# Group-norm statistics of layers 0 to 2 on ScalarE, layer 2's normalisation on ScalarE, and the quantiser's two steps swapped

## The chip, the cores and the metric

The kernel runs on one core of one Trainium2 chip. That core has a matrix engine (TensorE, "PE" in the profile), a vector engine (VectorE, "DVE"), a scalar engine (ScalarE, "ACT"), a general-purpose engine (GpSimd, "POOL", which does almost nothing here) and DMA queues, of which this kernel uses the one that SyncE ("SP") issues. Each engine takes its instructions in the order in which the program lists them and waits for the others by semaphores. The metric is the device time of one launch in microseconds, the median of three runs.

## The reference, cut to what matters

Eight images of 32 channels and 256 x 256 pixels in float32 go through four layers. Each adds its output to its input; the first three work on a group-normalised copy of it (16 groups of two channels, mean and variance over the whole image).

```
x: (8, 32, 256, 256) float32
def gn(v):  m, s = mean, var over each group of 2 channels;  return (v - m) / sqrt(s + 1e-5)

# layer 0: 1x1 convolution, then a depthwise 5x5 convolution whose weights are
#          the convolved feature map itself, average-pooled to 5x5
f = conv1x1(gn(x), w0) + b0;   x = x + depthwise5x5(f, adaptive_pool_5x5(f))
# layer 1: quantised "adder" convolution
q = round(clip(gn(x) / 2**-7, -127, 127));   wq = the same with the weights' own scale
x = x + -sum_{c, 3x3} |q patch - wq| * 2**-7        # for each of 32 outputs
# layer 2: 3x3 convolution
x = x + conv3x3(gn(x), w2) + b2
# layer 3: windows of 8x8, layernorm y, three small networks on three arrangements of y
#          (each: layernorm, eight Gaussians exp(-((v - g_k)/d)**2) times weights, plus
#          silu(v) times weights), their sum z, and a fourth such network on z
x = x + fastkan4(z) + z's residual
```

## The kernel before, in words

A pixel plane is cut into four bands of 64 rows; a tile has 128 partitions, band times channel. A chunk is eight rows of each band: 128 x 2048 values (`F` = 2048), eight chunks an image.

**Stage 0** (layer 0, from line 710). For each of eight chunks: a load from `x`, four `bn_stats` on DVE (`add_stats`, L618, the instruction is at L624) and five row sums for the pooled weights (L730). `Norm.finish` (L628) joins the statistics: `bn_aggr` (L637), two or three tiny matmuls across partitions, and a chain of small DVE operations. Then again for each chunk: a load with a border of two rows, 25 taps on PE (L873) and their edge corrections into the PSUM buffer `psB`, an eviction by ACT (L906), `bn_stats` for layer 1's normalisation, a store to `x1`. At the end eight tiles are scaled on ACT (L948), clipped (L953) and rounded to bf16 (L954) on DVE, and stored to `q`.

**Stage 1** (layer 1, L1008). Sixteen passes an image, one for each quarter of the rows and each group of eight output channels. A pass makes 72 distance tiles of 128 x 4128 values, max(q - w, 0), on DVE (L977) or, in halves, on ACT (L979), and PE sums each into the PSUM buffer `psA` (`gather`, L999: eight matmuls); nine more gathers take the plain sums, and one product adds the residual `xr` (L988). ACT evicts `psA` into `xr` (L1046), two `bn_stats` take the statistics for layer 2, a store goes to `x2`. Distance tiles have three buffers, `dv`.

**Stage 2** (layer 2, L1071). For each chunk: a load of ten rows, normalisation on DVE (`normal`, L1112), nine taps into `psB` (L1129), eviction by ACT (L1145), `bn_stats` for layer 3, a store to `x3`.

**Stage 3** (layer 3, L1170). Eight units an image, each one chunk through four networks. A network takes eight times a Square (L1368) and an Exp (L1381) on ACT and a product with weights on PE (L593) into `psB`; before it come a centring, a variance and a scaling that also go through PSUM (L1219, L1224, L1232, L1264, L1272). Line 1449 evicts the last network of a unit, so it runs 64 times.

**The order of the work** is made by a planner in the kernel itself (`Plan.run`, L228). It is a list schedule that runs while the program is built: every task has an engine, a cost in us, a rank (image plus a fraction) and buffers to be had, and a free engine takes the ready task of lowest rank. The time from one engine's end to another's start is `LAT`. Distances and gathers are not tasks but fillers (`fill`, L346; `Pass.piece`, L379; `on_pe`, L404): PE takes a gather ahead of all tasks when two distance tiles are waiting for it (`URGENT`), the other engines take a distance when no task is ready, and ACT only when it has had no task for 8 us (`IDLE`) or the image is the first. What comes out is one fixed instruction order for each engine. Ranks let stage 0 of later images, the passes of one image, and stages 2 and 3 of the image before run together. After the last pass, DVE may take Squares of stage 3 from ACT (L1374). The fixed memory `arena` (kind `sb`, ten times `F` words) holds most tiles; a load of a later image is only placed when five times `F` words stay free beyond its own (`FUTURE`).

```
            if self.sums and len(self.queue) < URGENT and (late or not (urgent or self.queue)):
                t, us, bufs, n = self.sums.pop(0), 0.53, [], 1
```

## Time and profile before

| | us |
|---|---|
| median of three runs (15972.1 to 15999.17) | 15973.13 |
| the profiled execution, its own time | 15969.78 |
| span in the profile, first to last instruction | 15967.3 |
| DVE busy | 13454.6 (84%) |
| PE busy | 12928.0 (81%) |
| ACT busy | 12386.4 (78%) |
| mean granted PE clock | 0.92 of full |
| DMA | mean 123 GB/s |

A busy time is the union of an engine's instructions. A row of the profile's groups names line, engine, operation and tiles ("out<-in"), the count, the busy time in us and the mean ns of one, and then the engine's idle time just ahead of such instructions with what ended it. The waits say who waited for whom: total us, times, longest. The windows give busy time in a stretch of the span, with the number of instructions behind an x.

The execution has five stretches, which show in the starts of the evictions at lines 1046, 1145 and 1449. Up to about 435 us there is only stage 0 of image 0. From there to 1,871 us come image 0's sixteen passes, beside stage 0 of images 1 to 3. To about 8,000 us the passes of images 1 to 4 run beside stage 3 of images 0 to 2 and stage 0 of the rest. To 14,602 us, the end of the last pass, stage 0 is over; passes run beside stages 2 and 3. The rest, 1,365 us, is the last of image 6's stage 3 (to 14,715 us) and then stages 2 and 3 of image 7 alone.

### The profile page before, as it was taken

To read this page: it belongs to the slowest core of one execution; us is meant where nothing else is said; L and a number is where in the kernel's file an instruction comes from. 1 tells how busy PE (TensorE), PEld (TensorE's weight loads), DVE (VectorE), ACT (ScalarE), POOL (GpSimd) and SP (SyncE) were. 2 spreads that over 40 slices of the span, in tenths; PEclk is the share of its full clock that TensorE was granted. 3 is DMA by queue.
4 is the path that set the end of the run, shared out by engine and by line. 5 is a ranking of instruction groups with operands and counts; after the bars stand their busy time and mean duration, and the time that the engine had idled before them with its cause. 6 is when DMAs were issued, how large, how long until landed. Compare 5 with 4: busy or idle time off the path is not lost. (4 is left out here: it accounts for less than half of the span.)

```text
span 15967.3 us, 560619 instructions
## 1 busy us (share of the span) xinstructions
PE 12928.0 (81%) x260296; PEld 4325.8 (27%) x260296; DVE 13454.6 (84%) x12544; ACT 12386.4 (78%) x6843; POOL 16.7 (0%) x25
## 2 busy tenths in 40 slices
PE   5889887987887888788887888788878888877666
PEld 4333322222332222232222222222222222222222
DVE  2889889898878889888999988999898989897465
ACT  0899749678658766866888987899779987997687
POOL 0000000000000000000000000000000000000000
PEclk8989899999999999899999999899999999998777
DMA  4332446445445444643554454444544454444554
GB/s 117 78 96 54 105 113 169 109 107 153 130 101 152 126 112 120 166 106 105 152 132 123 126 134 122 122 123 127 127 126 126 126 122 138 116 132 114 144 154 130
DMA packets 1192870, 1970.85 MB, mean 123 GB/s; under 512 B 362752, under 2 KB 878848, under 8 KB 1092224
## 3 DMA queue, kind: packets, MB, share of 16 engines
q1 hardware_dynamic: 1190528, 1934.98, 46.1%
q8 instruction: 2036, 33.36, 0.9%
q14 instruction: 306, 2.51, 0.1%
HBM read 1162.83 MB, written 771.75 MB: 121 GB/s over the span
## 5 line engine op out<-in xcount | busy, mean ns | idle before, releaser
L977 DVE TENSOR_SCALAR dv<-qh,w1q 128x4128 bf16<-128x4128 bf16 (+1 forms) x8831 | 10521.9, 1248 | 1376.3 <-PE psA L999 1319.3
L999 PE MATMUL psA<-dv,sel_b 128*32 128x512 bf16 x71240 | 5434.0, 405 | 1339.6 <-DVE dv L977 1054.2
L999 PEld LDWEIGHTS <-sel_b 128*32 128x32 bf16 x82944 | 2053.9, 97 | 6792.6 <-issue 5786.5
L1368 ACT ACTIVATE bas<-arena,kb 128x2048 f32<-128x2048 f32 x1386 | 2762.3, 1993 | 408.3 <-DVE arena L1272 262.9
L1381 ACT ACTIVATE bas<-bas 128x2048 f32<-128x2048 f32 x1386 | 2653.1, 1914 | 39.0
L979 ACT ACTIVATE dv<-qh,w1n 128x2064 bf16<-128x2064 bf16 x827 | 1628.6, 2009 | 1126.8 <-PE psA L999 1035.3
L593 PE MATMUL psB<-bas,tl 32*32 32x512 f32 x48416 | 1955.5, 652 | 491.1 <-ACT bas L1381 247.6
L873 PE MATMUL psB<-arena,wt 32*32 32x512 f32 (+1 forms) x51040 | 1848.5, 607 | 99.5 <-issue 61.4
L593 PE MATMUL psB<-arena,tl 32*32 32x512 f32 x22496 | 909.4, 621 | 161.7 <-ACT si L1449 46.1
L593 PEld LDWEIGHTS psB<-bas,tl 32*32 32x32 f32 x48416 | 535.2, 107 | 1384.3 <-ACT bas L1381 518.8
L873 PEld LDWEIGHTS psB<-arena,wt 32*32 32x32 f32 x51040 | 651.2, 104 | 778.1 <-issue 607.1
L1368 ACT ACTIVATE arena<-arena,kb 128x2048 f32<-128x2048 f32 x410 | 816.1, 1991 | 0.0
L1381 ACT ACTIVATE arena<-arena 128x2048 f32<-128x2048 f32 x410 | 785.0, 1915 | 12.3
L624 DVE BATCH_NORM_STATS2 tiny<-arena 128x6 f32<-128x512 f32 x768 | 473.5, 679 | 351.8 <-ACT arena L906 246.0
L999 PE MATMUL psA<-qh,sel_b 128*32 128x512 bf16 x9216 | 672.2, 393 | 92.3 <-DMA qh<-q 77.9
L1447 ACT ACTIVATE si<-psB,cols_sb 128x2048 f32<-128x2048 f32 x192 | 377.4, 1966 | 453.3 <-PE psB L593 369.9
L1272 DVE TENSOR_TENSOR arena<-psB,arena 128x2048 f32<-128x2048 f32 x280 | 640.5, 2287 | 86.2 <-PE psB L1264 79.2
L593 PE MATMUL psB<-si,tl 32*32 32x512 f32 x14080 | 630.6, 624 | 48.8 <-ACT si L1447 19.5
L1129 PE MATMUL psB<-arena,tl 32*32 32x512 f32 (+3 forms) x16384 | 626.6, 608 | 14.7 <-issue 14.4
L1224 ACT ACTIVATE arena<-arena 128x2048 f32<-128x2048 f32 x320 | 612.7, 1915 | 15.7 <-DMA x<-arena 5.8
L1264 PE MATMUL psB<-rs,tl 32*32 32x512 f32 x8960 | 338.9, 630 | 222.5 <-DVE arena L1272 128.2
L906 ACT ACTIVATE arena<-psB,cc 128x2048 f32<-128x2048 f32 x64 | 125.7, 1964 | 493.2 <-PE psB L894 493.2
(151 smaller groups left out, 7686.6 us busy)
## 6 DMA issues: line engine op xcount, KB each, us to landing
arena<-x SPq DMA_DIRECT2D x128, 1024.0 KB
arena<-y SPq DMA_DIRECT2D x128, 1024.0 KB
si<-sy SPq DMA_DIRECT2D x512, 256.0 KB
arena<-in_x_dram SPq DMA_DIRECT2D x240, 384.0 KB
arena<-in_x_dram SPq DMA_DIRECT2D x256, 256.0 KB
x<-arena SPq DMA_DIRECT2D x256, 256.0 KB
xr<-x SPq DMA_DIRECT2D x512, 128.0 KB
x<-xr SPq DMA_DIRECT2D x512, 128.0 KB
```

The source lines that it names most:

```text
L593: nc.tensor.matmul(o[j * C : (j + 1) * C, i - first, :], w_, src(rows, i, j), start=start, stop=stop)
L624: nc.vector.bn_stats(self.stats[:, at + i, :], a[:, i * 512 : (i + 1) * 512])
L873: nc.tensor.matmul(o[:, lo - 2 * j : hi - 2 * j, c0:c1], wt[rows, t, :], d[rows, lo + dy + 2 : hi + dy + 2, c0 + dx : c1 + dx], start=firs ...
L977: nc.vector.tensor_scalar(dst, src, w1q[:, at : at + 1], 0.0, ALU.subtract, ALU.max)
L979: nc.scalar.activation(dst, src, AF.Relu, bias=w1n[:, at : at + 1])
L999: nc.tensor.matmul(psA[j * C : (j + 1) * C, i, :], sel_b[:, n, :], src[:, at : at + 2, t % 3 : t % 3 + W], **flags,)
L1129: nc.tensor.matmul(o[:, lo - 2 * j : hi - 2 * j, c0:c1], (wc if t == 4 else tl[:, W2T + t, :])[rows], d[rows, lo + dy + 1 : hi + dy + 1, c ...
L1224: plan.add("ACT", 1.9, lambda: nc.scalar.activation(sb(sq), sb(c), AF.Square), r=[c], w=[sq], rank=rk)
L1272: lambda ps=ps, at=at: nc.vector.tensor_tensor(sb(c)[:, at], ps().rearrange("p s f -> p (s f)"), sb(c)[:, at], ALU.mult),
L1368: lambda k=k, bas=bas: nc.scalar.activation(sb(bas), sb(rb), AF.Square, bias=kb[:, n, k : k + 1]),
L1381: lambda k=k, bas=bas, square=square: nc.scalar.activation(sb(bas), sb(bas), AF.Exp, scale=-1.0, bias=0.0 if square.eng == "ACT" else kbsq ...
L1447: nc.scalar.activation(sb(o), psB.rearrange("p s f -> p (s f)"), AF.Identity, bias=obias)
```

## The change

**Statistics.** For the normalisations of layers 0, 1, 2 and 3 (every use of `bn_stats`), the sum is now taken by the instruction that writes the tile, where ACT writes it: the evictions at L906, L1046 and L1145 get `accum_out`. In stage 0's first part, where no ACT instruction writes the tile, DVE adds up the row sums that it makes anyway and takes off the columns that two bins share: three small operations. The sum of squares comes from a new ACT pass for each tile, `add_squares`: Square with a per-partition bias (minus the mean of the first tile, made by one small DVE operation for each group of tiles) and an accumulator; its elementwise output is bf16 waste, written behind the tile's data. So tiles get half as much room again: stage 0's first loads take 12 rows' worth instead of 8, stage 2's tiles 12 instead of 10, `xr` three quarters of `F` instead of half. `finish` replaces `bn_aggr` by six small DVE operations.

**Normalisation of layer 2.** `normal` is an Identity activation on ACT with scale and bias per partition, instead of a DVE `tensor_scalar`; one small DVE operation makes the bias.

**Quantiser.** DVE first rounds float32 to bf16 and then clips bf16 in place, instead of clipping in float32 and then rounding to bf16.

**Planner.** `LAT` grows by 0.03 to 0.05 us; a gather is costed at 0.49 instead of 0.53 us; PE pays 0.05 us in the plan each time it changes between fillers and tasks; tasks moved to ACT have costs there. A new rule lets PE take a gather instead of a task whose rank is over 9.0 (`AHEAD`) past the image of the current pass.

```diff
-ROOM = [("bas", 3 * BASE, BASE), ("si", 3 * F, F), ("rs", F // 2, F // 4), ("xr", F // 2, F // 2), ("sb", 10 * F, 0)]
+ROOM = [("bas", 3 * BASE, BASE), ("si", 3 * F, F), ("rs", F // 2, F // 4), ("xr", 3 * F // 4, 3 * F // 4), ("sb", 10 * F, 0)]
+AHEAD = 9.0
...
-    LAT = {"PE": 0.15, "DVE": 0.12, "ACT": 0.25, "SP": 2.0}
+    LAT = {"PE": 0.2, "DVE": 0.15, "ACT": 0.3, "SP": 2.0}
...
+                        if best is not None and e == "PE" and best.rank > self.image() + AHEAD:
+                            piece = self.fill(e, False)
+                            if piece is not None:
+                                best = piece
+                        if best is not None and best.n is not None:
...
+                    if e == "PE":
+                        us += 0.05 * ((t.n is None) != self.filling)
+                        self.filling = t.n is None
...
+    def image(self):
+        return next((p.b for p in self.passes[self.first_pass :] if not p.done), len(self.passes))
...
         if self.sums and len(self.queue) < URGENT and (late or not (urgent or self.queue)):
-            t, us, bufs, n = self.sums.pop(0), 0.53, [], 1
...
-            us, bufs, n = 0.53, [d], 1
+            us, bufs, n = 0.49, [d], 1
...
+            self.sums, self.squares, self.shift = t[:, 0:16], t[:, 16:32], t[:, 32 : 32 + n]
+            self.summed = Buf("fixed")
+            self.chunks, self.shifted = 0, [Buf("fixed") for _ in range(n)]
...
+        def add_squares(self, src, at, i, size, rank):
+
+            if not self.chunks & 1 << i:
+                self.chunks |= 1 << i
+                plan.add(
+                    "DVE", 0.16,
+                    lambda: nc.vector.tensor_scalar(
+                        self.shift[:, i : i + 1], self.sums[:, at : at + 1], -1.0 / size, None, ALU.mult
+                    ),
+                    r=[src, self.summed], w=[self.shifted[i]], rank=rank,
+                )
+            plan.add(
+                "ACT", 0.25 + 0.85e-3 * size,
+                lambda: nc.scalar.activation(
+                    sb(src)[:, size : size + size // 2].bitcast(BF16), sb(src, size), AF.Square, bias=self.shift[:, i : i + 1],
+                    accum_out=self.squares[:, at : at + 1],
+                ),
+                r=[src, self.shifted[i]], w=[self.bufs[at]], rank=rank,
+            )
...
             def first():
+                if self.chunks:
+                    mean, d, q = self.mv[:, :, 0], self.v, self.t
+                    for of, a in ((d, self.sums), (q, self.squares)):
+                        a = a[:, 0 : 2 * NH * n if n == 1 else NH * n].rearrange("p (n k) -> p n k", n=n)
+                        nc.vector.tensor_reduce(of, a, AX.X, ALU.add)
+                    count = float(HB * W // n)
+                    nc.vector.tensor_scalar(mean, d, 1.0 / count, None, ALU.mult)
+                    nc.vector.tensor_tensor(d, mean, self.shift, ALU.add)
+                    nc.vector.tensor_tensor(d, d, d, ALU.mult)
+                    nc.vector.scalar_tensor_tensor(self.mv[:, :, 1], q, 1.0 / count, d, ALU.mult, ALU.subtract)
+                    return
...
-            plan.add("DVE", 1.1 if n == 1 else 1.5, first, r=self.bufs, w=[small], rank=self.rank)
+            plan.add("DVE", 1.1 if n == 1 else 1.5, first, r=[*self.bufs, self.summed], w=[small], rank=self.rank)
...
+            xt = Buf("sb", 12 * W)
             plan.add(
-                "SP", 2.0, lambda k=k, xt=xt: by_block(lambda p, q: nc.sync.dma_start(sb(xt)[p], xn[k, q])),
+                "SP", 2.0, lambda k=k, xt=xt: by_block(lambda p, q: nc.sync.dma_start(sb(xt, F)[p], xn[k, q])),
...
             def pool(k=k, xt=xt):
-                v = sb(xt).rearrange("p (r w) -> p r w", w=W)
+                v = sb(xt, F).rearrange("p (r w) -> p r w", w=W)
...
-            norm.add_stats(xt, 4 * k, [], r(0.02 * k))
-            plan.add("DVE", 2.9, pool, r=[xt], w=[rs_buf[k]], rank=r(0.02 * k))
...
+                total, both = norm.sums[:, k : k + 1], norm.d[:, 0, 0:1]
+                nc.vector.tensor_reduce(total, rowsum[:, :, k * R : (k + 1) * R], AX.XY, ALU.add)
+                nc.vector.tensor_reduce(both, v[:, :, 51:205:51], AX.XY, ALU.add)
+                nc.vector.tensor_tensor(total, total, both, ALU.subtract)
...
+            plan.add("DVE", 3.4, pool, r=[xt], w=[rs_buf[k], norm.summed], rank=r(0.02 * k))
+            norm.add_squares(xt, k, 0, F, r(0.02 * k))
...
-                lambda xt=xt: nc.scalar.activation(
-                    sb(xt, F), psB.rearrange("p s f -> p (s f)"), AF.Identity, bias=bi
+                lambda k=k, xt=xt: nc.scalar.activation(
+                    sb(xt, F), psB.rearrange("p s f -> p (s f)"), AF.Identity, bias=bi,
+                    accum_out=norm1.sums[:, k : k + 1],
                 ),
...
-            norm1.add_stats(xt, 4 * k, [], rk)
+            norm1.add_squares(xt, k, 0, F, rk)
...
-                    nc.vector.tensor_scalar(sb(t, F), sb(t, F), QMAX, -QMAX, ALU.min, ALU.max)
+
                     nc.vector.tensor_scalar(q16(t), sb(t, F), ROUND, ROUND, ALU.add, ALU.subtract)
-
-                plan.add("DVE", 2.5, clip, w=[t], rank=rk)
+                    nc.vector.tensor_scalar(q16(t), q16(t), QMAX, -QMAX, ALU.min, ALU.max)
+
+                plan.add("DVE", 1.95, clip, w=[t], rank=rk)
...
-                ps.xr = xr = Buf("xr", F // 2)
+                ps.xr = xr = Buf("xr", 3 * F // 4)
...
                 gate = plan.add(
                     "ACT", 1.05,
-                    lambda g=g, xr=xr: nc.scalar.activation(
-                        sb(xr), psA.rearrange("p i f -> p (i f)"), AF.Identity, bias=wsum[:, g : g + 1]
+                    lambda g=g, h=h, xr=xr: nc.scalar.activation(
+                        sb(xr, F // 2), psA.rearrange("p i f -> p (i f)"), AF.Identity, bias=wsum[:, g : g + 1],
+                        accum_out=norm.sums[:, NH * g + h : NH * g + h + 1],
                     ),
...
-                norm.add_stats(xr, 8 * g + 2 * h, [], rk, 2)
+                norm.add_squares(xr, NH * g + h, g, F // 2, rk)
...
+        wc, b2, nmr = wt[:, K0 * K0 + 2, :], cc[:, 4:5], cc[:, 10:11]
...
+            nc.vector.scalar_tensor_tensor(nmr, norm.mean, -1.0, norm.rs, ALU.mult, ALU.mult)
...
         for k in range(NCH):
-            xt, p = Buf("sb", 10 * W), Buf("psB")
+            xt, p = Buf("sb", 12 * W), Buf("psB")
...
             def load(k=k, xt=xt):
-                d = sb(xt)
+                d = sb(xt, 10 * W)
...
             def normal(xt=xt):
-                nc.vector.tensor_scalar(sb(xt), sb(xt), norm.mean, norm.rs, ALU.subtract, ALU.mult)
-
-            plan.add("DVE", 1.7, normal, r=[norm.done], w=[xt], rank=rk)
+                nc.scalar.activation(sb(xt, 10 * W), sb(xt, 10 * W), AF.Identity, bias=nmr, scale=norm.rs)
+
+            plan.add("ACT", 2.4, normal, r=[sm["c2"]], w=[xt], rank=rk)
...
                 "ACT", 1.97,
-                lambda xo=xo: nc.scalar.activation(sb(xo, F), psB.rearrange("p s f -> p (s f)"), AF.Identity, bias=b2),
+                lambda k=k, xo=xo: nc.scalar.activation(
+                    sb(xo, F), psB.rearrange("p s f -> p (s f)"), AF.Identity, bias=b2,
+                    accum_out=norm3.sums[:, k : k + 1],
+                ),
                 r=[p, sm["c2"]], w=[xo], rank=rk,
...
-            norm3.add_stats(xo, 4 * k, [], rk)
+            norm3.add_squares(xo, k, 0, F, rk)
```

## The prediction

> **What bounds the kernel now.** I read the page's totals first, then its groups, then the windows cut at the five stretches named above, then the waits in the two long stretches, and last the timeline where an engine looked full. The totals, and the groups that the change touches:
>
> ```profile
> PE 12928.0 (81%) x260296; PEld 4325.8 (27%) x260296; DVE 13454.6 (84%) x12544; ACT 12386.4 (78%) x6843; POOL 16.7 (0%) x25
> ...
> L977 DVE TENSOR_SCALAR dv<-qh,w1q 128x4128 bf16<-128x4128 bf16 (+1 forms) x8831 | 10521.9, 1248 | 1376.3 <-PE psA L999 1319.3
> ...
> L979 ACT ACTIVATE dv<-qh,w1n 128x2064 bf16<-128x2064 bf16 x827 | 1628.6, 2009 | 1126.8 <-PE psA L999 1035.3
> ...
> L624 DVE BATCH_NORM_STATS2 tiny<-arena 128x6 f32<-128x512 f32 x768 | 473.5, 679 | 351.8 <-ACT arena L906 246.0
> ```
>
> No engine is full over the span; three are nearly level. DVE leads, and most of what it does is distances. ACT makes some of these too, as a filler, at 2.0 us for a half that costs DVE 0.645. By stretch (columns: length, then busy us of PE, PEld, DVE, ACT, POOL):
>
> ```profile
> 435.00:1871.00 1436.00, 1258.03 (x26022) 475.13 (x26014) 1278.71 (x1563) 1293.51 (x681) 2.13 (x2) 0.91 0.33 80
> 1871.00:8000.00 6129.00, 5175.09 (x109201) 1683.40 (x109202) 5312.16 (x5103) 4356.95 (x2386) 4.86 (x6) 0.95 0.48 127
> 8000.00:14602.00 6602.00, 5369.81 (x101586) 1679.69 (x101569) 5991.80 (x5058) 5721.52 (x3172) 8.56 (x7) 0.93 0.47 126
> 14602.00:14842.00 240.00, 161.32 (x3702) 80.79 (x3702) 99.27 (x100) 103.36 (x56) 0.00 (x0) 0.81 0.53 130
> 14842.00:15967.30 1125.30, 724.10 (x12870) 242.13 (x12870) 640.48 (x350) 877.15 (x533) 0.00 (x0) 0.75 0.52 143
> ```
>
> I call the first three B, C and D. B: all three engines at 88 to 90%. C: DVE 87%, PE 84%, ACT only 71%. D: DVE 91%, ACT 87%, PE 81%. What DVE lacks to 100% is mostly a wait for PE to free a distance buffer (waits in C, then in D):
>
> ```profile
> DVE dv L977 <- PE psA L999: 708.5, 735, 22.1
> PE psA L999 <- DVE dv L977: 329.3, 561, 9.0
> ...
> PE psA L999 <- DVE dv L977: 714.5, 1230, 5.9
> DVE dv L977 <- PE psA L999: 526.9, 629, 11.9
> ```
>
> In C, PE holds DVE up more than the reverse; in D it is the other way round. In C stage 3 and stage 0 also share one accumulator, `psB`: the windows give 2813 us of PE, 550 of ACT and 266 of DVE on it, 59% of the stretch before counting the gathers that run in between. And in D, inside stage 3, ACT is full (timeline, ACT alone):
>
> ```profile
> 12512.67 1.92 ACT L1381 ACTIVATE bas<-bas 128x2048 f32<-128x2048 f32 x1
> 12514.49 1.99 ACT L1368 ACTIVATE bas<-arena,kb 128x2048 f32<-128x2048 f32 x1
> 12516.50 1.92 ACT L1381 ACTIVATE bas<-bas 128x2048 f32<-128x2048 f32 x1
> ```
>
> So two chains run to the end. The passes end at 14,602, set by DVE and PE. Stage 3 goes unit by unit from image 0 to image 7, psB-bound in C and ACT-bound in D (units end at 12,170 and 12,348: 178 us); image 6's ends at 14,715, only 113 us after the last pass. Image 7's stages 2 and 3 need both and last to the end, 141 us a unit.
>
> **What the skill says.** The Trainium skill, "ScalarE: Activation LUTs", *What ACT_TABLE_LOAD costs*: an ACTIVATE with a pointer bias takes about 280 ns plus 0.833 ns an element, each further pointer 93 ns more. The trace agrees: 1993 ns at L1368, 2086 at L948 with bias and scale. "VectorE: DVE Perf Modes", *The perf-mode tier table*: float32 `tensor_scalar` on 2048 values 1227 ns, bf16 693, `tensor_reduce` always at the lowest rate. The trace has 1222 (L953), 1227 (L954) and 750 for 2064 bf16 values with a pointer (L977). "Perfetto Trace Analysis", *Identifying the Most-Contended Engine*: work first on the engine of highest occupancy. Here that is DVE, but by 3 points over PE. No page that I found prices ScalarE's accumulator output.
>
> **The change, part by part.**
>
> Taken from DVE: `bn_stats`, 635 us in the windows of L624 (52 before B, 107 in B, 310 in C, 146 in D, 21 after). `normal`, 103 us (48 in C, 42 in D, 13 after). The quantiser: 64 x (1.22 + 1.23) becomes 64 x (1.23 + 0.69), 34 us less. Given to DVE: 64 x 3 small operations on 32 to 40 values, at some 0.19 each (the smallest reduce at L766 is 0.197, small operations 0.16): 36 us; 56 shifts at 0.16, 9 us; one operation in stage 2, 1 us. `bn_aggr` (24 x 1.01 + 32 x 0.26) against 32 x 6 x 0.17: even. Net 726 us off DVE.
>
> Given to ACT: 192 Squares of 2048 at 1.99 = 382; 128 of 1024 at 0.28 + 0.85 = 1.13, 145; 64 normalisations of 2560 at 2.086 + 0.43 = 2.51, 161. Accumulators on 320 Squares and 256 evictions: no row shows one. At best free, at worst a small operation's fixed part, 0.2 us (L1249 takes 0.631 for 512 values, 0.427 of it elements); I take 0.1, 58 us, ends 0 and 115. Together 746 (688 to 803). No table loads: Square and Identity run between others at L1224 and L1447 with none ahead of them.
>
> So the change moves some 730 us from DVE to ACT, one for one. Where does it come through?
>
> *B.* DVE loses 107 + 8 - 13 = 102; ACT gains 36 Squares and 15 half ones with accumulators, 96. ACT makes 1215 us of distances here and hands some back: at unchanged shares, ACT 1389.5 - 2m = 0.90 T and DVE 1176.7 + 0.645m = 0.89 T give T = 1377, 59 us less. PE would be at 91%; I take 50.
>
> *C.* DVE loses 310 + 48 + 19 - 20 - 5 = 352. ACT has 1772 us idle, so its 360 more fit. But 709 of DVE's 817 idle us wait for PE, whose work stays. I let two fifths through: 150.
>
> *D.* DVE loses 188; ACT gains 204 and gives up its last 109 us of distances (54 halves, 35 us of DVE): 153 net. DVE mostly leads here; three quarters, 115. The passes end 315 earlier, about 14,287.
>
> *Stage 3's chain.* It starts after image 0's passes: 50 earlier. In C nothing for it. In D 61 Squares of `xr` with accumulators, 75 us, come onto a full ACT: I count 60 back; stage 2's 120 us fall where ACT waits at the change of image. So at 14,287 it stands 10 behind: 438 us to go, at 178 a unit. Without passes, and with DVE taking Squares, it goes at 141: 347, so it ends near 14,634. Stage 2 of image 7 then no longer stands alone between 14,715 and 14,842 but runs beneath; I count 50 for its claim on `psB`. The first unit of image 7 took 256 us from 14,842; its start can overlap too, 60 less. End: 14,634 + 50 + 1125 - 60 = 15,749 of span.
>
> *The rest.* Head: `psB`'s 25 taps set it; ten `F` words hold six of the larger tiles instead of ten, but loads follow one another at DVE's pace. Nothing; if the cover fails, one load, some 5 us. Stage 2's `normal` in line on ACT behind a 2 us Square: 8 x 2 us at the end if loads are late, in the range. Larger tiles in `arena` make stage 0 of later images wait for more free room; it ends 4,600 us before it is needed, so delay costs nothing and may ease `psB` in C. `AHEAD` = 9.0 never acts: ranks stay under 9. The costs fit better: a lone gather and a product alternate every 1.62 us in the timeline (14565.49 to 14567.11), the plan had 0.53 + 1.03, now 0.49 + 1.03 + 2 x 0.05 = 1.62. That moves order only; some 60 us either way, not in the sum.
>
> The span stands 2.5 us under its run and the run 3.4 under the median, so I forecast 15,750 (223 less, 1.4%).
>
> **The rivals.**
>
> *Both ledgers bind.* If the passes and stage 3 only need DVE and ACT time, B to D together (DVE 12,583 of 14,167, ACT 11,372) lose 643 and gain 661; with m halves handed back, 12,583(1 - p) = 12,583 - 643 + 0.645m and 11,372(1 - p) = 11,372 + 661 - 2m give p = 2.65%, 375 us, and some overlap at the end: 15,560. For it: ACT's 71% in C. Against: DVE's waits for PE there. With DVE alone the bound, 643/0.888 = 724 less, 15,250: the floor, which PE's 84% in C excludes.
>
> *Only the passes gain.* Stage 3 is the later chain already; if image 7's overlap fails (110 of the gain) and D costs it the whole 75, the end comes at 15,880 to 16,000. For it: ACT full in D. Against: the last pass and stage 3 lie 113 us apart.
>
> *Slower.* Place: ACT's line between the Exps of stage 3. A Square for statistics put there by rank delays an Exp, holds `psB` 2 us longer and with it everything that waits for `psB`. From C on ACT gains 564 us; if some 280 of them (my 223 plus the 60 already counted) land in such holds, the gain is gone; with 400, 16,090. For it: ACT is strictly in order. Against: 1772 idle us in C.
>
> **Chances.** My forecast's case, 15,640 to 15,890: 0.48. Both ledgers, below it: 0.24. Only the passes, 15,890 to 16,005: 0.14, half of it under 15,941. Slower, to 16,200: 0.14. A measurement of this kernel can tell about 0.2%, 32 us. Faster 0.79, same 0.07, slower 0.14. For 8 in 10 the range leaves out the ends of the first rival and of the last: 15,470 to 16,030.
>
> **What would show it.** DVE busy near 12,730 plus 0.645 for each half that ACT hands back, ACT near 13,130 less 2.0 for each, of the 973 it makes now; Squares of 1.99 and 1.13 us, normalisation 2.51; passes ending near 14,290, image 6's stage 3 some 350 later, image 7's stage 2 before that. Wrong if: an accumulating ACTIVATE shows a second instruction above 0.2 us; waits for PE in C grow by as much as DVE's work shrinks; stage 3's units in D grow from 178 to over 185; or passes end early and stage 3 ends where it did.

## The result, and the profile after

The kernel after takes 15,854.03 us (median of four runs, 15,846.96 to 15,881.44) against 15,973.65 for the kernel before (four runs, 15,972.1 to 15,999.17): ratio 0.9923, 95% interval 0.9909 to 0.9938. That is 120 us or 0.8% less; the forecast was 223 us less. The profiled execution of the kernel after took 15,848.52 us, with a span of 15,846.7 against 15,967.3.

The totals of the kernel after (busy us, share of the span, instructions):

```profile
PE 12834.1 (81%) x260296; PEld 4256.1 (27%) x260296; DVE 13020.2 (82%) x11996; ACT 12681.7 (80%) x7588; POOL 26.6 (0%) x25
```

From its groups, the rows of the lines that moved (L1032 and L1034 are the distances, before at L977 and L979):

```profile
L1032 DVE TENSOR_SCALAR dv<-qh,w1q 128x4128 bf16<-128x4128 bf16 (+1 forms) x8831 | 10536.7, 1252 | 1415.7 <-PE psA L1054 1370.0
...
L1034 ACT ACTIVATE dv<-qh,w1n 128x2064 bf16<-128x2064 bf16 x686 | 1354.5, 2010 | 1050.3 <-PE psA L1054 1021.2
...
L656 ACT ACTIVATE arena<-arena,tiny 128x2048 bf16<-128x2048 f32 x192 | 383.5, 1998 | 70.7 <-DMA arena<-in_x_dram 43.0 <-DVE tiny L649 25.1
...
L1169 ACT ACTIVATE arena<-arena,cc,tiny 128x2560 f32<-128x2560 f32 x64 | 160.3, 2512 | 15.8 <-DMA arena<-x 5.7 <-DMA x<-xr 5.5 <-DVE dv L1032 4.5
L656 ACT ACTIVATE xr<-xr,tiny 128x1024 bf16<-128x1024 f32 x128 | 146.0, 1140 | 2.1 <-DVE tiny L649 0.8
...
L1008 DVE TENSOR_SCALAR arena<-arena 128x2048 bf16<-128x2048 f32 x64 | 78.3, 1223 | 24.0 <-ACT arena L1002 23.6
L1009 DVE TENSOR_SCALAR arena<-arena 128x2048 bf16<-128x2048 bf16 x64 | 44.5, 695 | 2.2
L656 ACT ACTIVATION_READ_ACCUMULATOR arena<-arena,tiny 128x1 f32 x192 | 36.0, 188 | 0.0
```

The work moved as the prediction priced it: Squares of 2.00 and 1.14 us, a normalisation of 2.51, a clip of 0.695 instead of one of 1.22. (The 192 Squares of 2,048 columns are those of layers 0, 1 and 3. Layer 3, too, works on a group-normalised copy, which the title and the cut reference leave out.) DVE has 434 us less and ACT 295 more. The windows, cut at the kernel after's own last passes of image 0 (1,656) and image 7 (13,946), with the columns of the prediction's windows:

```profile
435.00:1656.00 1221.00, 1124.77 (x23308) 386.14 (x23298) 1167.68 (x1371) 1180.95 (x695) 1.61 (x2) 0.94 0.29 70
1656.00:8000.00 6344.00, 5347.26 (x110414) 1734.28 (x110418) 5478.62 (x5149) 4895.30 (x2959) 13.71 (x7) 0.96 0.49 128
8000.00:13946.00 5946.00, 4916.66 (x96608) 1556.76 (x96600) 5313.22 (x4600) 5046.41 (x2987) 10.16 (x6) 0.95 0.48 127
13946.00:14721.00 775.00, 465.19 (x10068) 172.87 (x10068) 336.35 (x211) 597.98 (x347) 0.00 (x0) 0.76 0.51 136
14721.00:15846.70 1125.70, 732.96 (x12864) 236.83 (x12864) 634.96 (x323) 876.91 (x533) 0.00 (x0) 0.74 0.51 143
```

In B, the first row, all three engines now stand at 92 to 97%. The fourth row is the new one: 775 us between the last pass and the end of image 6's stage 3, in which DVE is busy for 43% and PE for 60%. Before, this gap was 113 us. The waits in C and in D of the kernel after follow. Before, DVE waited 709 and 527 us for PE, and PE 329 and 715 us for DVE; so in C each now waits more for the other, and in D PE waits less for DVE:

```profile
DVE dv L1032 <- PE psA L1054: 775.1, 757, 23.9
...
PE psA L1054 <- DVE dv L1032: 460.8, 788, 8.5
...
DVE dv L1032 <- PE psA L1054: 563.8, 622, 45.1
PE psA L1054 <- DVE dv L1032: 555.6, 970, 5.5
```

Where the 120 us are is seen in five instructions of ACT's timeline. In the kernel before: the last pass's eviction, the last of image 6's stage 3, the first and last eviction of image 7's stage 2, and the first unit of image 7's stage 3 (start us, duration):

```profile
14601.76 1.12 ACT L1046 ACTIVATE xr<-psA,wsum 128x1024 f32<-128x1024 f32 x1 [0.23 <-PE psA L999]
14710.67 3.92 ACT L1449 ACTIVATE si<-psB,cc 128x2048 f32<-128x2048 f32 x1 [4.45 <-PE psB L593]
14725.80 1.97 ACT L1145 ACTIVATE arena<-psB,cc 128x2048 f32<-128x2048 f32 x1 [11.21 <-PE psB L1129]
14837.18 1.97 ACT L1145 ACTIVATE arena<-psB,cc 128x2048 f32<-128x2048 f32 x1 [11.47 <-PE psB L1129]
15098.15 3.99 ACT L1449 ACTIVATE si<-psB,cc 128x2048 f32<-128x2048 f32 x1
```

The same five in the kernel after:

```profile
13946.14 1.09 ACT L1101 ACTIVATE xr<-psA,wsum 128x1024 f32<-128x1024 f32 x1
14212.79 1.95 ACT L1202 ACTIVATE arena<-psB,cc 128x2048 f32<-128x2048 f32 x1
14677.42 1.97 ACT L1202 ACTIVATE arena<-psB,cc 128x2048 f32<-128x2048 f32 x1 [1.91 <-PE psB L1186]
14711.61 3.92 ACT L1509 ACTIVATE si<-psB,cc 128x2048 f32<-128x2048 f32 x1 [8.98 <-PE psB L604]
14978.51 3.95 ACT L1509 ACTIVATE si<-psB,cc 128x2048 f32<-128x2048 f32 x1 [0.74 <-PE psB L604]
```

The passes end 656 us sooner. Image 6's stage 3 ends at the same time, 14,715 and 14,716. Because the passes are over, image 7's stage 2 (L1145, now L1202) runs beneath image 6's stage 3 instead of behind it, and the first unit of image 7 ends 120 us sooner. From there to the end both take 858 us. So DVE's relief reached the passes, and of 656 us only 120 reached the end.

**The middle of the run.** Stage 3 did not simply stay where it was. Windows of single lines show it (stretch, ACT's busy us with the number of instructions, clock, DMA). In the kernel before, the evictions of stage 0's chunks (L906, 64 in all; the count holds one table load more) up to 8,000 us:

```profile
0.00:8000.00 8000.00, 126.96 (x65) 0.94 0.46 119
```

and those of stage 3's units (L1449), up to 8,000 us and on to 13,300:

```profile
0.00:8000.00 8000.00, 85.98 (x21) 0.94 0.46 119
8000.00:13300.00 5300.00, 111.42 (x27) 0.93 0.48 126
```

In the kernel after, the same chunks (L959, now two records each, so 52 chunks and 12):

```profile
0.00:8000.00 8000.00, 106.71 (x104) 0.95 0.46 119
8000.00:14716.00 6716.00, 24.62 (x24) 0.93 0.48 128
```

and the units of the kernel after (L1509):

```profile
0.00:8000.00 8000.00, 98.04 (x24) 0.95 0.46 119
8000.00:13300.00 5300.00, 94.09 (x23) 0.95 0.48 127
```

By 8,000 us the kernel after is three units of stage 3 ahead and twelve chunks of stage 0 behind. Both stages accumulate in `psB`. I added up in both traces how long `psB` is held, each time from the first matmul into it to the end of the instruction that empties it, cut at the ends of the stretch:

| 435 to 8,000 us, us of `psB` held | before | after |
|---|---|---|
| stage 0's convolutions | 2851 | 2383 |
| stage 3 | 3339 | 3726 |
| stage 2's convolutions | 498 | 569 |
| together, these three | 6688 | 6678 |
| share of the stretch, everything | 0.90 | 0.90 |
| share, 8,000 to 10,770 us | 0.81 | 0.91 |
| share, 10,770 to 13,947 us | 0.82 | 0.82 |
| share, 13,947 to 14,716 us | 0.82 | 0.99 |

Up to 8,000 us the accumulator was held for the same time in both kernels. Stage 3's lead at 8,000 us was borrowed from stage 0, and it was paid back by 10,770: there both kernels end the same unit, the third of image 4 (10,768 before, 10,773 after).

The later units of stage 3 end at these times (us):

| unit | before | after |
|---|---|---|
| image 4, third | 10768 | 10773 |
| image 5, third | 12352 | 12358 |
| image 5, last | 13249 | 13330 |
| image 6, third | 13938 | 13970 |
| image 6, seventh | 14630 | 14586 |
| image 6, last | 14715 | 14716 |
| image 7, first | 15102 | 14982 |

Up to the last pass (13,947 us) stage 3 keeps nearly the pace that it had before, with `psB` held for 0.82 of the time in both kernels. Image 5's last units come later while stage 2 of image 6 uses `psB` earlier (its eight evictions end from 12,426 to 12,988 us, before from 13,015 to 13,265); most of that is made up again by the third unit of image 6, which ends 32 us later. After the last pass `psB` is full: it is held for 0.99 of the 769 us up to the end of image 6, and 119 us of that belong to stage 2 of image 7. So the last five units of image 6 take 746 us, against 777 in the kernel before, where passes run beside them.

### The profile page after: what moved, and what is told of

Same layout as the page of the kernel before. It is cut to its first block, busy times and chain, and to the rows that moved or that the text cites. A ratio compares the mean times of both kernels' runs of the same rounds, so it can differ in the third digit from the quotient of the medians.

```text
span 15846.7 us, 560546 instructions
## 1 busy us (share of the span) xinstructions
PE 12834.1 (81%) x260296; PEld 4256.1 (27%) x260296; DVE 13020.2 (82%) x11996; ACT 12681.7 (80%) x7588; POOL 26.6 (0%) x25
## 3 DMA queue, kind: packets, MB, share of 16 engines
q14 instruction: 306, 2.51, 0.1%
## 4 chain that ended last, share of the span: by engine, by line
PE 26%; ACT 26%; DVE 7%; issue 6%; DMA 1%; SPq 0%; ACTq 0%; DVEq 0%
PE psB L604 8%; PE psA L1054 8%; ACT bas L1441 7%; ACT bas L1428 7%; PE psB L926 4%; DVE dv L1032 3%; PE psB L1186 3%; ACT arena L1279 2%; ACT arena L1441 2%; ACT arena L1428 2%; DVE arena L1332 1%; ACT si L1507 1%; ACT si L1509 1%; ACT arena L1284 1%; DVE arena L1434 1%
## 5 line engine op out<-in xcount | busy, mean ns | idle before, releaser
L1032 DVE TENSOR_SCALAR dv<-qh,w1q 128x4128 bf16<-128x4128 bf16 (+1 forms) x8831 | 10536.7, 1252 | 1415.7 <-PE psA L1054 1370.0
L1054 PE MATMUL psA<-dv,sel_b 128*32 128x512 bf16 x70800 | 5329.6, 400 | 1215.5 <-DVE dv L1032 1032.1
L1428 ACT ACTIVATE bas<-arena,kb 128x2048 f32<-128x2048 f32 x1410 | 2810.2, 1993 | 322.1 <-DVE arena L1332 257.7
L1441 ACT ACTIVATE bas<-bas 128x2048 f32<-128x2048 f32 x1410 | 2698.8, 1914 | 39.7
L604 PE MATMUL psB<-bas,tl 32*32 32x512 f32 x51040 | 2049.3, 652 | 539.0 <-ACT bas L1441 252.8
L1034 ACT ACTIVATE dv<-qh,w1n 128x2064 bf16<-128x2064 bf16 x686 | 1354.5, 2010 | 1050.3 <-PE psA L1054 1021.2
L604 PE MATMUL psB<-arena,tl 32*32 32x512 f32 x19872 | 818.6, 625 | 211.5 <-ACT si L1509 87.9
L1054 PE MATMUL psA<-qh,sel_b 128*32 128x512 bf16 x9216 | 672.1, 387 | 83.0 <-DMA qh<-q 73.4
L1186 PE MATMUL psB<-arena,tl 32*32 32x510 f32 (+3 forms) x16384 | 620.4, 609 | 9.0 <-issue 8.9
L1284 ACT ACTIVATE arena<-arena 128x2048 f32<-128x2048 f32 x320 | 613.0, 1916 | 9.7
L1434 DVE SCALAR_TENSOR_TENSOR bas<-arena,kb 128x2048 f32<-128x2048 f32 x185 | 429.2, 2349 | 192.6 <-PE psB L604 170.1
L1428 ACT ACTIVATE arena<-arena,kb 128x2048 f32<-128x2048 f32 x293 | 583.3, 1991 | 1.7 <-PE psB L604 1.4
L1441 ACT ACTIVATE arena<-arena 128x2048 f32<-128x2048 f32 x293 | 560.8, 1914 | 8.4
L959 ACT ACTIVATE arena<-psB,cc 128x2048 f32<-128x2048 f32 x64 | 125.6, 1963 | 510.9 <-PE psB L947 510.9
```

What stands on the lines that cost most here:

```text
L604: nc.tensor.matmul(o[j * C : (j + 1) * C, i - first, :], w_, src(rows, i, j), start=start, stop=stop)
L1032: nc.vector.tensor_scalar(dst, src, w1q[:, at : at + 1], 0.0, ALU.subtract, ALU.max)
L1034: nc.scalar.activation(dst, src, AF.Relu, bias=w1n[:, at : at + 1])
L1054: nc.tensor.matmul(psA[j * C : (j + 1) * C, i, :], sel_b[:, n, :], src[:, at : at + 2, t % 3 : t % 3 + W], **flags,)
L1186: nc.tensor.matmul(o[:, lo - 2 * j : hi - 2 * j, c0:c1], (wc if t == 4 else tl[:, W2T + t, :])[rows], d[rows, lo + dy + 1 : hi + dy + 1, c ...
L1284: plan.add("ACT", 1.9, lambda: nc.scalar.activation(sb(sq), sb(c), AF.Square), r=[c], w=[sq], rank=rk)
```

## The experiments

Four theories. **P**: stage 3's chain through `psB` sets image 6's end, and DVE only sets when the passes end. **D**: DVE's (or ACT's) time sets the end. **A**: what ACT took over eats what DVE gave up. **C**: the planner's new costs carry the gain. A fifth, **R**, says that the larger tiles and the late stage 0 cost the rest. The table has the median, the ratio to the kernel before with its interval, and from each profile the end of the last pass, of image 6's stage 3, the start of the last eviction of image 7's stage 2, and the ends of image 7's first and last unit, in us.

| kernel | median | ratio | passes | image 6 | stage 2 | first | last |
|---|---|---|---|---|---|---|---|
| before | 15973.65 | | 14603 | 14715 | 14837 | 15102 | 15960 |
| after | 15854.03 | 0.9923 [0.9909, 0.9938] | 13947 | 14716 | 14677 | 14982 | 15840 |
| e7 thin bn_stats, on before | 15883.12 | 0.9942 [0.9925, 0.9958] | 14080 | 14767 | 14728 | 15028 | 15882 |
| e1 new costs, on before | 16038.28 | 1.0036 [1.0023, 1.0049] | 14685 | 14776 | 14893 | 15161 | 16029 |
| e4 larger tiles, on before | 15975.49 | 0.9997 [0.9988, 1.0005] | 14649 | 14729 | 14847 | 15111 | 15968 |
| e2 old costs, on after | 15893.31 | 0.9948 [0.9933, 0.9963] | 13989 | 14762 | 14723 | 15024 | 15882 |
| e3 cheap Squares, on after | 15893.73 | 0.9942 [0.9927, 0.9957] | 14040 | 14762 | 14722 | 15025 | 15894 |
| e5 bn_stats in stage 0, on after | 15924.96 | 0.9964 [0.9951, 0.9977] | 14064 | 14782 | 14744 | 15045 | 15916 |
| e6 normalisation on DVE, on after | 15856.60 | 0.9920 [0.9905, 0.9934] | 14166 | 14707 | 14719 | 14987 | 15849 |
| e8 fewer taps, on after | 15411.56 | 0.9640 [0.9624, 0.9656] | 14133 | 14131 | 14274 | 14541 | 15410 |
| e12 no plain sums, on after | 15856.58 | 0.9927 [0.9912, 0.9942] | 14040 | 14756 | 14718 | 15019 | 15882 |
| e9 one more base, on after | 15828.47 | 0.9906 [0.9892, 0.9921] | 14201 | 14639 | 14683 | 14947 | 15815 |
| e10 bases and Squares, on after | 15796.65 | 0.9892 [0.9876, 0.9909] | 14186 | 14627 | 14652 | 14918 | 15790 |

From the first unit of image 7 to the last it is 854 to 872 us in every kernel. From image 6's end to that first unit it is 382 to 410 where image 7's last stage 2 eviction starts 117 us or more behind image 6's end, 261 to 267 where it starts some 38 us ahead of it, and 280 to 308 where it starts 12 to 44 us behind. The rest is image 6's end.

**DVE alone relieved (e7).** In the kernel before, each `bn_stats` reads 16 of its 512 columns.

```diff
-                    nc.vector.bn_stats(self.stats[:, at + i, :], a[:, i * 512 : (i + 1) * 512])
+                    nc.vector.bn_stats(self.stats[:, at + i, :], a[:, i * 512 : i * 512 + 16])
...
-            plan.add("DVE", 0.69 * n, fn, ...
+            plan.add("DVE", 0.18 * n, fn, ...
```

> The kernel before, with bn_stats on 16 of each 512 columns (the statistics are wrong; everything else is computed). DVE loses about 460 us, ScalarE gets nothing. Theory P (the end is set by stage 3's chain, which runs through PE and the one accumulator psB; DVE only sets the end of the passes): passes end some 400 to 700 us earlier, near 13,900 to 14,200, image 6's stage 3 still near 14,700, time 15,800 to 15,900. Theory D (DVE and ScalarE time bound, as in my rival of both ledgers): 460/0.89 = 515 less, about 15,450. Theory A (the work put on ScalarE eats what DVE gives): without that work clearly faster than the changed kernel, 15,500 to 15,650.

Measured: 15,883.12 against 15,981.73 for the kernel before in the same measurement, 99 us less (91 against the table's first row). The rows of this kernel, where before had 473.5 and 163.8 us of `bn_stats`:

```profile
L624 DVE BATCH_NORM_STATS2 tiny<-arena 128x6 f32<-128x16 f32 x768 | 77.1, 163 | 461.1 <-ACT arena L906 258.9 <-ACT arena L1145 155.7 <-DMA arena<-in_x_dram 43.6
...
L624 DVE BATCH_NORM_STATS2 tiny<-xr 128x6 f32<-128x16 f32 x256 | 31.9, 166 | 37.0 <-ACT xr L1046 36.5
```

528 us leave these rows and no work of the statistics comes onto ACT. DVE's total falls by only 333 us (13,121.5 for 13,454.6), mostly because DVE takes 77 more Squares of stage 3 from ACT after the last pass; ACT's falls by 155. The passes end 523 us sooner, and the end comes 99 sooner, inside P's band. So D falls, which asked for 515, and A too: without one new Square on ACT the gain is no larger than the change's own. `psB` is held for 0.99 from the last pass to image 6's end here as well.

**ACT alone relieved (e3).** In the kernel after, the statistics' Squares read an eighth of their columns.

```diff
-                "ACT", 0.25 + 0.85e-3 * size,
+                "ACT", 0.25 + 0.85e-3 * size / 8,
...
-                    sb(src)[:, size : size + size // 2].bitcast(BF16), sb(src, size), AF.Square, ...
+                    sb(src)[:, size : size + size // 16].bitcast(BF16), sb(src, size // 8), AF.Square, ...
...
-                    nc.vector.scalar_tensor_tensor(self.mv[:, :, 1], q, 1.0 / count, d, ALU.mult, ALU.subtract)
+                    nc.vector.scalar_tensor_tensor(self.mv[:, :, 1], q, 8.0 / count, d, ALU.mult, ALU.subtract)
```

> The kernel after, with each Square of the statistics over an eighth of its columns (the sum of squares is then taken times eight; the variance is an estimate, the rest of the work is whole). That takes about 380 us off ACT and leaves DVE, PE and the order's rules alone. Theory A (the work that the change put on ACT eats what DVE gives up, one for one): 250 us or more below the kernel after, under 15,600. Theory P: only the share that falls between the Exps of stage 3 and 0 to 75 us of it, 15,780 to 15,850. Theory D (the passes and their DVE time set the end): some 150 us from distances that ACT takes back, 15,700.

Its rows, 383.5 and 146.0 us in the kernel after:

```profile
L656 ACT ACTIVATE arena<-arena,tiny 128x256 bf16<-128x256 f32 x192 | 96.5, 503 | 87.9 <-DMA arena<-in_x_dram 62.1 <-DVE tiny L649 23.0
L656 ACT ACTIVATE xr<-xr,tiny 128x128 bf16<-128x128 f32 x128 | 50.3, 393 | 2.1 <-DVE tiny L649 0.7
```

383 us leave these rows. ACT's total falls by 290 (12,391.8 for 12,681.7), since it makes 32 more halves of distances and leaves fewer Squares to DVE. The end comes 40 us later, not sooner. All theories missed the sign; A, which asked for 250 us, is refuted a second time. P had allowed a small gain for the part of ACT's work that sits between the Exps of stage 3: not seen.

**Normalisation back on DVE (e6).**

```diff
-                nc.scalar.activation(sb(xt, 10 * W), sb(xt, 10 * W), AF.Identity, bias=nmr, scale=norm.rs)
+                nc.vector.tensor_scalar(sb(xt, 10 * W), sb(xt, 10 * W), norm.mean, norm.rs, ALU.subtract, ALU.mult)
...
-            plan.add("ACT", 2.4, normal, r=[sm["c2"]], w=[xt], rank=rk)
+            plan.add("DVE", 1.7, normal, r=[norm.done], w=[xt], rank=rk)
```

> The kernel after, with layer 2's normalisation back on DVE: ACT loses 160 us, DVE gains 103. Theory P: within 60 us of the kernel after, 15,800 to 15,910. Theory A: 100 us or more less, under 15,750. Theory D: 80 us more, 15,930.

15,856.60 against 15,854.03: no difference. The passes end 219 us later, and the end does not need those 219 us: image 6 ends at 14,707 against 14,716. This part of the change is worth nothing at the end.

**The planner's costs, alone and undone (e1, e2).** The same lines of the diff, put into the kernel before and taken out of the kernel after:

```diff
-    LAT = {"PE": 0.15, "DVE": 0.12, "ACT": 0.25, "SP": 2.0}
+    LAT = {"PE": 0.2, "DVE": 0.15, "ACT": 0.3, "SP": 2.0}
...
+                    if e == "PE":
+                        us += 0.05 * ((t.n is None) != self.filling)
+                        self.filling = t.n is None
...
-            t, us, bufs, n = self.sums.pop(0), 0.53, [], 1
+            t, us, bufs, n = self.sums.pop(0), 0.49, [], 1
...
-            us, bufs, n = 0.53, [d], 1
+            us, bufs, n = 0.49, [d], 1
```

> The kernel before with the planner's new costs alone (LAT, a gather at 0.49, 0.05 for a change between fillers and tasks). Theory P, D and A: order only, within 60 us of before, 15,910 to 16,030. If the costs carry the change (theory C): near 15,850, and image 0's passes end near 1,660 instead of 1,871.

> The changed kernel with the planner's old costs. Theory P, D and A: within 60 us of the changed kernel, 15,790 to 15,915, and image 0's passes still end near 1,660. Theory C: the gain is gone, near 15,970, and those passes end near 1,870.

Alone, the costs make the kernel before 0.36% slower, 8 us beyond the band of P, D and A; in the kernel after they are worth 39 us. The two signs differ, so C isn't the carrier. The other sign agrees: image 0's passes end at 1,877 us in e1 and at 1,666 in e2, against 1,871 before and 1,656 after (and at 1,669 in e7, with DVE relieved alone). Both times image 6's end moves, by 61 and 46 us, with work unchanged: that is the size of what a mere other order did here.

**The room (e4).** The kernel before with the larger tiles:

```diff
-ROOM = [..., ("xr", F // 2, F // 2), ...]
+ROOM = [..., ("xr", 3 * F // 4, 3 * F // 4), ...]
...
-            xt = Buf("sb", F)
+            xt = Buf("sb", 12 * W)
...
-            xt, p = Buf("sb", 10 * W), Buf("psB")
+            xt, p = Buf("sb", 12 * W), Buf("psB")
```

> The kernel before with the larger tiles alone (12 rows for stage 0's first loads and stage 2, three quarters of F for xr). If the room is what put stage 0 of images 5 to 7 off from 8,300 us to 10,600 us, its last quantiser tile comes after 9,500 here too. Theory P: moving that work along the span moves the end little, 15,880 to 16,030. If room is a loss of its own (theory R): 16,030 to 16,150, and the change would have been worth that much more without it.

No difference (15,975.49, twelve runs). The last scaling on ACT for image 7's quantiser (L948) starts at 8,974 us against 8,312 before and 10,593 in the kernel after, so the room explains only part of the late stage 0. It is not a loss of its own, so R's first half falls.

**Stage 0 early again (e5).** In the kernel after, stage 0's first statistics by `bn_stats` on tiles of eight rows.

```diff
-            xt = Buf("sb", 12 * W)
+            xt = Buf("sb", F)
...
-                total, both = norm.sums[:, k : k + 1], norm.d[:, 0, 0:1]
-                ...
-            plan.add("DVE", 3.4, pool, r=[xt], w=[rs_buf[k], norm.summed], rank=r(0.02 * k))
-            norm.add_squares(xt, k, 0, F, r(0.02 * k))
+            norm.add_stats(xt, 4 * k, [], r(0.02 * k))
+            plan.add("DVE", 2.9, pool, r=[xt], w=[rs_buf[k]], rank=r(0.02 * k))
```

> The kernel after, with stage 0's first statistics by bn_stats on tiles of 8 rows, as before: DVE gets 165 us back, ACT loses 130, and stage 0 needs less room. Theory P: stage 0 takes the same time in psB whenever it runs, so within 60 us of the kernel after, 15,790 to 15,910, even if stage 0 of images 5 to 7 ends a thousand us sooner. Rival (theory R, the late stage 0 took stage 3's lead): stage 0 of image 7 ends before 9,500 and the end comes 100 to 250 us sooner, 15,600 to 15,750.

The last scaling for image 7's quantiser starts at 9,477 us, 1,116 sooner than in the kernel after. The end comes 71 us later, just outside P's band and on the far side of R's. By 8,000 us this kernel has ended 22 units of stage 3 and 56 chunks of stage 0, between the kernel before (21 and 64) and the kernel after (24 and 52); the third unit of image 4 ends at 10,787 us, within 19 us of both. When stage 0 runs does not decide, as the table of holds says.

**The accumulator (e8) against PE's time (e12).** First 12 of 25 taps left out in stage 0 of images 1 to 7; then the nine gathers of the plain sums left out of each pass of images 1 to 7.

```diff
-        tap_order = [mid * K + mid] + [t for t in range(K * K) if t != mid * K + mid]
+        tap_order = [mid * K + mid] + [t for t in range(K * K) if t != mid * K + mid][: 24 if b == 0 else 12]
```

> The kernel after, with 13 of the 25 depthwise taps in stage 0 of images 1 to 7; it leaves out 12 taps for each of 56 chunks, about 700 us of PE work and of psB's time, and nothing of DVE or ACT. Theory P (the end is set by stage 3's chain through PE and its one accumulator psB, with stages 0 and 2 in the same queue): 350 to 600 us less than the kernel after, 15,250 to 15,500. Theories D and A (DVE's or ACT's time sets the end): both keep their work, so under 100 us less, 15,750 or more.

```diff
-        self.sums = list(range(9))
-        self.left = 9 + OG * 9
+        self.sums = list(range(0 if b else 9))
+        self.left = len(self.sums) + OG * 9
...
```

> The kernel after, with the nine gathers of the plain sums left out of each pass of images 1 to 7 (the outputs of layer 1 lack that term): 112 passes x 9 x some 0.45 us, about 450 us of PE less, none of it in psB. It tells PE's time from the hold of its accumulator. Theory P in the form 'psB is the queue' (stage 3, stage 0 and stage 2 take turns in one accumulator, and PE's time outside it matters only where it falls into a hold): under 120 us less, 15,740 to 15,850. Theory P in the form 'PE's time is the bound': 440 us came from 700 in the run with fewer taps, so some 280 here, 15,570. Theories D and A: under 60 us.

The totals of e8:

```profile
PE 12311.9 (80%) x238862; PEld 4043.3 (26%) x238862; DVE 12797.8 (83%) x11852; ACT 12689.5 (82%) x7598; POOL 41.7 (0%) x25
```

and of e12:

```profile
PE 12587.6 (79%) x252232; PEld 4046.8 (25%) x252232; DVE 12999.0 (82%) x11983; ACT 12687.8 (80%) x7590; POOL 22.8 (0%) x25
```

e8 takes 522 us off PE and the end comes 442 us sooner, inside P's band. e12 takes 247 off PE's busy time (less than the 450 that I had expected, and the row of the plain sums alone falls by 583 us, from 672.1 to 89.1; the granted clock of both profiles was 0.913, against 0.925 in the kernel after). In proportion to e8 that would be 247 x 442 / 522 = 209 us. It brought none: 15,856.58. (PE's busy time on `psB` grew from 6,622 to 6,688 us in e12, which may hide a gain of that order, not one of 209.) So PE's time outside `psB` does not count at the end, and its time in `psB` does. Two things are not told apart by this pair: the taps left out in e8 hold `psB`, and they also stand in the list of tasks in which PE makes stage 3's products, while e12's gathers are fillers. No run gave stage 3 an accumulator of its own, which would tell them apart. In e8, a chunk of stage 0 holds `psB` for 31 us on average instead of 53 up to 8,000 us; the accumulator is held for 0.84 of that stretch instead of 0.90, and stage 0 is over by then with stage 3 a unit further. Image 6 ends 585 us sooner, at the same time as the passes (14,131 and 14,133 us), and image 7's stage 2 is exposed again, which costs 144 (410 less 266): 585 - 144 = 441.

**More Gaussians in store (e9), and a looser rule for starting and sharing them (e10).**

```diff
-BASE_SPARE = 3 * F
+BASE_SPARE = 2 * F
```

> The kernel after, with the free room that is kept before stage 3 may take one more tile for its Gaussians cut from three times 2048 words to twice (BASE_SPARE); no work is added or taken away. ACT can then prepare one Gaussian further ahead of the product on PE that frees it, so psB's holds get shorter. Theory P: 60 to 150 us less than the kernel after, 15,700 to 15,800, stage 3's units in the second half under 188 us. Theories D and A: within 40 us of the kernel after.

```diff
-IDLE = 8.0
+IDLE = 6.0
...
-BASE_SPARE = 3 * F
-HOLD = 4
+BASE_SPARE = 2 * F
+HOLD = 3
...
-                            if t.eng != e and not all(p.done for p in self.passes[self.first_pass :]):
+                            if t.eng != e and self.image() < t.rank + 0.5:
```

> The kernel after, with one tile more for stage 3's Gaussians (as in the run with one more base), a product that may start when three instead of four of them are ready (HOLD), ACT free for distances after 6 us without a task instead of 8, and DVE allowed to take Squares of stage 3 from ACT once the passes stand half an image past them. No work is added. Theory P: shorter holds of psB and a quicker last image, 60 to 150 us below the kernel after, 15,700 to 15,800. Theories D and A: more of DVE's time goes to Squares while it is the bound, so 0 to 100 us more.

e9 is 26 us under the kernel after; the intervals overlap and P's 60 was missed. e10 is 57 us under it, just short of what P expected, and the intervals just touch (0.9876 to 0.9909 against 0.9909 to 0.9938). They end image 6 77 and 89 us sooner and give 42 and 25 of it back at image 7's start, where their stage 2 ends after image 6 instead of before it. e10 beats both kernels: 1.1% under the kernel before.

## Why the prediction was right in direction and too large

*Bookkeeping: right.* DVE was to be near 12,730 plus 0.645 for each half that ACT hands back, ACT near 13,130 less 2.0 for each. ACT makes 122 halves fewer (851 against 973), so 12,809 and 12,886. Measured 13,020 and 12,682. The difference is one thing that was left out: the passes end so early that DVE takes 93 more Squares of stage 3 (345 against 252), 93 x 2.35 = 219 us onto DVE and 93 x 1.99 = 185 off ACT, which makes 13,028 and 12,701. (The forecast's last step is off by 5 us: the two offsets that it names, 2.5 and 3.4, make 15,755 of 15,749, not 15,750.)

*The accumulator output: right at 0.1 us, and looks like twice that.* Each of the 576 accumulating instructions shows a second one of 0.19 us, 109.6 us in all. But rows of ACT overlap, as three successive ones of the kernel after show:

```profile
11698.31 1.11 ACT L1101 ACTIVATE xr<-psA,wsum 128x1024 f32<-128x1024 f32 x1 [0.32 <-PE psA L1054]
11699.32 0.19 ACT L1101 ACTIVATION_READ_ACCUMULATOR xr<-psA,wsum 128x1 f32 x1
11699.41 1.90 ACT L1441 ACTIVATE bas<-bas 128x2048 f32<-128x2048 f32 x1
```

From start to next start, where nothing waits, the eviction takes 1.09 us with the accumulator and 1.00 without (L1046 before), a Square of 2048 1.99 against 1.89: 0.09 to 0.10 us each, so some 55 us against 58 predicted.

*The passes: right sign, half the size.* "315 earlier, about 14,287" was 656. B gave 215 (1,656 for 1,871) instead of 50: waits went there that I had taken to stay, PE's 78 us for one load, 125 us for ACT's halves (now 36) and DVE's 84 for PE (now 32). e7 has nearly the same gain there, 202 us, from DVE's relief alone. C and D gave the rest, 441 against 265. "I let two fifths through" in C took DVE's waits for PE as fixed by PE's work. They grew a little (709 to 775 us), and the passes still took 441 of the 505 us that the prediction had DVE lose in C and, net, in D.

*Stage 3's chain up to the last pass: near in sum, by an exchange that was not foreseen.* The prediction had the chain 50 us earlier from B, nothing in C and 60 back in D, so 10 behind when the passes end. Measured, it is three units ahead at 8,000 us, 5 us behind at 10,773 and 32 behind at 13,970. "In C nothing for it" is right on balance only: three units were gained there against twelve chunks of stage 0. The delay of stage 0 was costed at nothing ("it ends 4,600 us before it is needed, so delay costs nothing and may ease `psB` in C"). That is true for the passes, but each late chunk holds `psB` for some 48 us in D, where the kernel before had no chunk left. This took back the whole lead, with the 50 of B in it. From there to the last pass 27 us were lost, not 60.

*The steps that failed: stage 3's pace after the last pass, and the start of image 7.* "Without passes ... it goes at 141", with 50 for stage 2's claim on `psB`: but 141 us is the mean of image 7's units (its first with its start, the next six 125 to 130 us each), beside which no stage 2 runs. With one beneath, the fourth to seventh unit of image 6 took 154 us each and the last 130; `psB` was held for 0.99 of that time, 119 us of it by stage 2. At the prediction's own pace, from 32 us behind at 13,947, with the 800 us that were then left at the pace of the kernel before, image 6 would have ended at 13,947 + 800 x 141 / 178 + 50 = 14,631 (an estimate from its terms); it ended at 14,716, 85 later. "Its start can overlap too, 60 less" did not come about: the first unit of image 7 ends 267 us after image 6, where the sum has 256 - 60 = 196, so 71 more. Against these stands that the passes ended 341 us sooner than forecast: the same sum from 14,287 has 14,634 + 50 = 14,684, so 53 less. With 5 less for the rest of image 7, 85 + 71 - 53 - 5 = 98 us, by which the span of 15,847 missed 15,749.

*Image 7: the sum right by luck, the overlap right.* 50 + 1,125 - 60 = 1,115 us from image 6's end to the end of the span; measured 15,847 - 14,716 = 1,131. But the 50 falls before image 6's end, where stage 2 now runs, and the 60 did not come: the two nearly cancel. What was foreseen rightly is that stage 2 of image 7 runs beneath image 6. From image 6's end to that of the first unit it is 267 us instead of 387, and these 120 us are the whole gain.

*The rivals.* "Only the passes gain" described the mechanism better than the forecast: stage 3 is the later chain, and the lead that it has at the end of C is gone by 10,770 us. Its other half, that image 7's overlap fails, did not come true; had it, the time would have been the kernel before's. "Both ledgers bind" falls with e7 and e3: neither DVE's nor ACT's time sets the end. "Slower" named the right place, `psB`'s holds, but the wrong holder: not Squares for statistics between the Exps (e3 takes most of them away for nothing) but stage 0's convolutions up to 10,770 us and stage 2's after the last pass. The Trainium skill's "Perfetto Trace Analysis", *Identifying the Most-Contended Engine*, led to DVE by occupancy; in e7, 528 us taken from its rows brought 99. (The same section says that matmul busy time is not a good measure for TensorE, so "by 3 points over PE" says less than it seems.) What was held for 0.93 of C in the kernel before was no engine but a buffer, and the prediction had seen 59% of it as engine time and stopped there.

*What stays open.* Edits that should have changed nothing or helped (e2, e3, e5) came out 39 to 71 us above the kernel after, all by image 6's end (14,762 to 14,782 against 14,716). A list schedule answers each edit with another order; how much of the kernel after's 120 us is such luck, these runs don't say exactly. But six kernels with other orders whose passes also end early (e2, e3, e5, e6, e7 and e12) lie 49 to 117 us below the kernel before, so it is not all luck. The swap of the quantiser's steps (34 us of DVE) and the rule `AHEAD` were not run alone. What sets stage 3's pace between 10,770 us and the last pass, where `psB` is held for 0.82 of the time, was not found: neither DVE's relief (e7) nor ACT's (e3) nor PE's outside `psB` (e12) quickened it. Nor was it found why a network's products of stage 3 hold `psB` for 28 us between 8,000 and 10,770 us in the kernel after and for 25.5 before.

## What to carry to other kernels

Before crediting a relieved engine, add up how long each shared accumulator or buffer is held, from first write to release, gaps included, and do so for each stretch. Here the stretch that decided, from the last pass to the end of image 6, had one buffer held for 0.99 of it while the busiest engine stood at 77%. A lead that one stage gains in such a buffer may be borrowed from another that uses it, so count both at the same time. Work that comes free early is worth what it lets overlap at the end, here one stage of 120 us out of 656, and what is overlapped takes its place in the shared buffer.

## What the runs showed of the hardware

An ACTIVATE with an accumulator output is followed by a separate ACTIVATION_READ_ACCUMULATOR of 188 to 194 ns, which the prediction had only bounded; it overlaps its neighbours, so it lengthens ACT's line by 0.09 to 0.10 us. A `bn_stats` on 16 values takes 163 ns against 679 for 512, so 516 ns more for 496 more values, 1.04 ns each.
